# Joins between the steps of the first stage, products ahead in the opening of the product-key stage, and the states of the first batch kept on chip

## The chip, the cores and the metric

The kernel runs on one core of one Trainium2 chip. The metric is the device time of one execution in microseconds (us); the time of a kernel is the median over its runs. TensorE multiplies matrices, VectorE and ScalarE do elementwise work and reductions, GpSimd does elementwise work and issues transfers whose rows are chosen by data, SyncE (SP) issues most other transfers, and ScalarE issues some of them. All values are float32; in the profile each matrix product of the program stands as two TensorE instructions, and "products" below counts those.

## The reference

Two layers follow each other, each of the form `x = x + ffn(cond(x))`, on x of 16 batches, 256 tokens and 256 features (N = 4096 tokens). Cut to what matters here:

```python
# layer 0, cond: a shared gated net and two of eight experts for each token
shared = silu(xf @ w1) * (xf @ w3) @ w2
s = sigmoid(concat([xf, t_emb]) @ router_W)          # the two largest of s + router_bias are chosen
y0 = (shared + sum_of_two(gate * (gelu(xf @ W1e[e]) @ W2e[e]))) / 3
# layer 0, ffn: product keys, 8 heads, 8 of 64 x 64 pairs of keys for each head
xn = (y0 - mean) * rsqrt(var + eps) * gamma + beta    # mean and var over ALL tokens
sim = einsum(xn @ w_q.T, keys)                        # 2 x 8 heads x 64 scores
idx, scores = top 8 of the 64 sums of the top 8 of either half
o = gelu(y0 . key_in[idx]) * softmax(scores);  x1 = x + o @ key_out[idx]
# layer 1, cond: a recurrent net over the 256 tokens of each batch (gates i, f, o, g) -> z
# layer 1, ffn: attention on z, then two of eight experts for each token; x1 + result
```

The mean and the variance over all tokens stand between the first stage and the product keys: no choice of keys can begin before the last token of y0 is there.

## The kernel before, in words

**Order.** The Python functions are generators that emit instructions; `steps(gen, n)` lets one emit up to its n-th next `yield`. When the program is built, a scheduler fixes the order on each engine: among the instructions whose inputs and buffers it expects to be ready, it takes the one that stands earliest in the emitted text. So an instruction can run well ahead of its place in the text (the load of `gam`, line 558, left at 0.7 us), and one that stands late is put off while earlier ones keep its engine busy. On the chip each engine runs its fixed order and waits where an input is late.

**First stage (to 474.7 us).** y0 is held transposed in `y` (also called `sh`), in 8 blocks of 512 tokens. `route(c)` (line 325 on) handles 1024 tokens: the logits `lg` (335), Sigmoid (342), the choice of two experts, and 16 scattered transfers of rows to `axd` (`send`, line 323), through two buffers `row`. `shared(blk)` (416 on) computes the shared net of a block in four steps: h1 = w1 x (423), h3 = w3 x (426), Tanh (428), two VectorE instructions to `gt` (429, 431), and at once the products of `gt` with w2 into `acc` (433). Line 436 writes the result into `sh`. Routing chunk c runs beside block 2c. After the four chunks stand, in the text, the loads of gamma, beta, `kin` and `kout` (the product-key tables, 4 MB each, in four pieces each, 558 to 564, from ScalarE's queue), then `listing`, `shared(1)` and the 71 expert tiles of `routed`. Those tiles (192 to 372 us) scatter their results into `ayd`.

**Joins (371.9 to 474.7 us).** `join(blk)` (217 on) goes through the four groups of 128 tokens of a block: it loads the two expert results of each token from `ayd` (222, SP, three buffers `r`), sums them on GpSimd (224), transposes the sum (227) and adds it to `sh` (229). Then it stores the block to `yd` (232, ScalarE's queue), takes the statistics (234) and copies the first 16 tokens of each batch to `y0` (235). In the text: `shared(3)` with steps of `fold` (which prepares the keys `wk`, 584 to 590), joins 0, 1, 2, `shared(5)` with `fold`, joins 3, 4, 5, `shared(7)`, joins 6, 7.

**Product-key stage (to 2401 us).** 32 chunks of 128 tokens (8 tokens of each of 16 batches). For chunk u, `select_experts(u)` makes scores `sp` (715), the top 8 (725, 726), the pairs (738, 739), and turns the result to `chosen` (773, 777), in eight steps; `weights_of` builds the dense weights `w` of the chunk in eight steps (VectorE 793, 794, 796; TensorE 801 into the single buffer `wp`; ScalarE 805); `experts(u, w, xt)` has eight steps of 16 products `po` with `kin` (820), Gelu to `ge` (825), the multiplication with `w` (826) and 16 products `acc` with `kout` (829). `recur(v)` is the recurrent net over the eight tokens of the chunk before (897 to 916), which writes the states `zt`. `wts` has two buffers, and so have `po` and `ge`.

The opening does all of `select_experts(0)`, `weights_of` of chunk 0 and `select_experts(1)`. The loop over u then takes, eight times, one step each of `experts(u)`, `weights_of` for u + 1, `select_experts(u + 2)` and `recur(u - 1)`. Each second chunk the states go to memory, `zd` (999).

**Attention and second experts (2401 us on).** For each batch b, `front(b)` reads its states z from `zd` (1029, four buffers); `ends(b)` is the last to use them (1273, 1279).

Of the kernel before, what the change touches and what calls it, by code (L numbers as in the profile page):

```python
# [8 lines left out]
F32 = mybir.dt.float32  # L9
# [152 lines left out]
def adaln_ffn_kernel(ctx: ExitStack, tc: tile.TileContext, i: dict, out: bass.AP):  # L162
# [54 lines left out]
    def join(blk):  # L217

        for u in range(blk * TBLK // P, (blk + 1) * TBLK // P):
# [9 lines left out]
            nc.vector.tensor_tensor(sh[:, :, cols], sh[:, :, cols], pj, ALU.add)  # L229
        nb = TBLK // T  # L230
# [6 lines left out]
    with (  # L237
# [76 lines left out]
        now = {"count": count}  # L314

# [12 lines left out]
        def route(c):  # L328
# [13 lines left out]
            nc.scalar.activation(s, s, AF.Sigmoid)  # L342
# [73 lines left out]
        def shared(blk, xb=None):  # L416

            xb = xb or load_x(blk)
            acc = [pacc.tile([P, TBLK], F32, name=f"acc{d}", tag=f"acc{d}") for d in range(KC)]
            for c in range(HS // P):  # L420
                h1 = pmm.tile([P, TBLK], F32, name="h1", tag="mm")
                for k in range(KC):
                    nc.tensor.matmul(h1, w1[:, k, c * P : (c + 1) * P], xb[:, k, :], start=(k == 0), stop=(k == KC - 1))
                h3 = pmm.tile([P, TBLK], F32, name="h3", tag="mm")
# [7 lines left out]
                for d in range(KC):  # L432
                    nc.tensor.matmul(acc[d], w2[:, c, d * P : (d + 1) * P], gt, start=(c == 0), stop=(c == HS // P - 1))
                yield
            for d in range(KC):
                nc.scalar.mul(sh[:, d, blk * TBLK : (blk + 1) * TBLK], acc[d], 1.0 / 3.0)
# [121 lines left out]
        nc.scalar.dma_start(out=gam, in_=i["gamma"])  # L558
        nc.scalar.dma_start(out=bet, in_=i["beta"])
        for q in range(4):  # L560
            w = NE // 4
            nc.scalar.dma_start(out=kin[:, :, q * w : (q + 1) * w], in_=i["kinT"][:, :, q * w : (q + 1) * w])
            w = NC // 4
            nc.scalar.dma_start(out=kout[:, q * w : (q + 1) * w], in_=i["kout"][:, q * w : (q + 1) * w])
# [28 lines left out]
        with tc.tile_pool(name="cf", bufs=2) as cf:  # L593
            fd = fold(cf, ptr)
            for n, blk in enumerate((3, 5, 7)):
                sh_ = shared(blk)
                for _ in range(HS // P):
                    steps(sh_, 1)
                    steps(fd, 1 if n < 2 else 0)
                steps(sh_)  # L600
                if n == 0:
                    for b_ in (0, 1, 2):
                        join(b_)
                elif n == 1:
                    for b_ in (3, 4, 5):
                        join(b_)
            steps(fd)
            for b_ in (6, 7):
                join(b_)
# [13 lines left out]
    with tc.tile_pool(name="cw", bufs=1) as cw:  # L623
# [32 lines left out]
        lnw = fw.tile([P, 4, KC], F32, name="w_ln")  # L656
        wqk = fw.tile([P, 2, KC, D], F32, name="wqk")
        with (
# [153 lines left out]
            def experts(u, w, xt):  # L812

                acc = [pacc.tile([P, P], F32, name=f"acc{d}") for d in range(KC)]
                yu = of_tile(yt[u // XT], u % XT)
                for c in range(0, NC, CQ):
                    po = pmm.tile([P, CQ, P], F32, name="po", tag="mm")
                    for h in range(CQ):
                        for k in range(KC):
                            nc.tensor.matmul(  # L820
                                po[:, h, :].rearrange("p (b t) -> p b t", t=SPC), kin[:, k, (c + h) * P : (c + h + 1) * P], yu[:, k],
                                start=(k == 0), stop=(k == KC - 1),
                            )
                    ge = ct.tile([P, CQ, P], F32, name="ge")
                    nc.scalar.activation(ge, po, AF.Gelu)  # L825
                    nc.vector.tensor_tensor(ge, ge, w[:, c : c + CQ, :], ALU.mult)  # L826
# [93 lines left out]
            def new_w(u):  # L920
# [704 lines left out]
```

## Time and profile before

| | us |
|---|---|
| median of 3 runs | 3642.41 |
| lowest, highest | 3628.58, 3655.81 |
| profiled execution | 3655.55 |
| its span in the profile | 3653.4 |
| mean granted TensorE clock | 0.953 |

| stretch | from | to |
|---|---|---|
| routing, shared blocks 0, 2, 4, 6, 1 | 0 | 192 |
| 71 expert tiles | 192 | 371.9 |
| shared blocks 3, 5, 7, joins, keys | 371.9 | 474.7 |
| opening of the product-key stage, and chunk 0 | 474.7 | 588 |
| chunks 1 to 31 | 588 | 2355 |
| recurrent net of the last chunk, alone | 2355 | 2401 |
| attention and second experts | 2401 | 3653.4 |

How to read it: the profile is of one execution. An engine's busy share is an average over stages with different limits, so each stage is read from the wait that ends last in it. In a line of the time line stand start, length, engine, line of the kernel, operation, output<-inputs, count, and in brackets the idle time before it and what ended it. PE is TensorE, PEld its loading of weights, DVE is VectorE, ACT is ScalarE, POOL is GpSimd. A `q` behind an engine's name is its issuing of transfers. Buffer numbers are left out of names.

### The profile page before, as it was taken

To read this page: it belongs to the slowest core of one execution; us is meant where nothing else is said; L and a number is where in the kernel's file an instruction comes from. 1 tells how busy PE (TensorE), PEld (TensorE's weight loads), DVE (VectorE), ACT (ScalarE), POOL (GpSimd) and SP (SyncE) were. 2 spreads that over 40 slices of the span, in tenths; PEclk is the share of its full clock that TensorE was granted. 3 is DMA by queue.
4 is the path that set the end of the run, shared out by engine and by line. 5 is a ranking of instruction groups with operands and counts; after the bars stand their busy time and mean duration, and the time that the engine had idled before them with its cause. 6 is when DMAs were issued, how large, how long until landed. Compare 5 with 4: busy or idle time off the path is not lost.

```text
span 3653.4 us, 72829 instructions
## 1 busy us (share of the span) xinstructions
PE 3407.6 (93%) x26776; PEld 2584.4 (71%) x26776; DVE 2282.4 (62%) x7358; ACT 1492.2 (41%) x3700; POOL 669.4 (18%) x1148
## 2 busy tenths in 40 slices
PE   7899869999999999999999999869999999999896
PEld 4467447777777777777777777635577777777796
DVE  3433378888787887878888787335555646455323
ACT  1133125455454544545455454333343444443221
POOL 3545220000000000000000000101222222222221
PEclk9999969999999999999999999967799999999997
DMA  6233430111101111011111101130133333232666
GB/s 232 95 106 107 146 72 13 33 27 30 36 16 36 22 36 33 19 36 22 36 23 29 36 19 30 33 116 24 52 102 115 103 117 103 99 102 97 199 218 219
DMA packets 423359, 273.05 MB, mean 75 GB/s; under 512 B 304800, under 2 KB 381472, under 8 KB 412384
## 3 DMA queue, kind: packets, MB, share of 16 engines
q1 hardware_dynamic: 397776, 208.21, 21.1%
q0 software_dynamic: 13344, 36.60, 2.7%
q10 hardware_dynamic: 11888, 23.60, 1.9%
q8 instruction: 216, 3.54, 0.4%
q14 instruction: 135, 1.11, 0.1%
HBM read 191.88 MB, written 76.44 MB: 73 GB/s over the span
## 4 chain that ended last, share of the span: by engine, by line
PE 73%; DVE 9%; DMA 6%; issue 5%; ACT 4%; POOL 2%; SPq 0%; ACTq 0%; DVEq 0%; POOLq 0%
PE acc L829 13%; PE po L820 9%; PE gp L897 7%; PE wp L801 7%; PE g L1458 6%; PE g L1445 5%; PE sp L715 3%; PE bp L853 3%; PE sc L1209 3%; PE ph L517 2%; PE mm L1237 2%; PE py L531 2%; DVE i L726 1%; DVE s L725 1%; DMA axd<-row,slot 1%
## 5 line engine op out<-in xcount | busy, mean ns | idle before, releaser
L829 PEld LDWEIGHTS acc<-ge,kout 128*128 128x128 f32 x4096 | 485.3, 193 | 93.9 <-DVE ge L826 47.5
L820 PEld LDWEIGHTS po<-yt,kin 128*128 128x128 f32 x3840 | 458.9, 191 | 105.8 <-issue 105.0
L829 PE MATMUL acc<-ge,kout 128*128 128x128 f32 x4096 | 525.5, 281 | 6.4 <-DVE ge L826 4.9
L820 PE MATMUL po<-yt,kin 128*128 128x128 f32 x3840 | 508.0, 281 | 0.0
L805 ACT COPY wts<-wp 64x256 f32<-64x256 f32 x1024 | 375.2, 366 | 187.5 <-PE wp L801 174.9
L916 POOL TENSOR_SCALAR zt<-hT 128x32 f32<-128x32 f32 x256 | 118.9, 465 | 1530.7 <-DVE hT L915 1403.3
L897 PE MATMUL gp<-wh,hT 128*32 128x256 f32 x4096 | 318.9, 393 | 30.6 <-DVE hT L915 22.1
L796 DVE TENSOR_TENSOR oh<-chosen,parted 128x1024 f32<-128x1024 f32 x256 | 311.8, 1218 | 0.0
L801 PE MATMUL wp<-oh,ol 128*64 128x128 f32 x4096 | 300.3, 284 | 9.7 <-ACT wts L805 9.6
L1449 ACT ACTIVATE hT<-g,b 128x128 f32<-128x128 f32 x284 | 104.7, 369 | 431.4 <-DVE hT L1451 367.4
L1458 PE MATMUL g<-mw,hT 128*128 x1136 | 272.9, 395 | 6.8 <-ACT xT L1435 3.5
L1445 PE MATMUL g<-xT,w 128*128 128x128 f32 x2272 | 274.7, 276 | 1.2 <-DVE ys L1463 1.2
L1445 PEld LDWEIGHTS g<-xT,w 128*128 128x128 f32 x2272 | 269.1, 192 | 6.0 <-DVE ys L1463 1.6
L801 PEld LDWEIGHTS wp<-oh,ol 128*64 128x64 f32 x4096 | 229.6, 139 | 59.7 <-issue 15.7
L1458 PEld LDWEIGHTS g<-mw,hT 128*128 128x128 f32 x1136 | 220.9, 200 | 43.6 <-ACT xT L1435 8.5
L825 ACT ACTIVATE ge<-po 128x512 f32<-128x512 f32 x256 | 151.8, 593 | 216.2 <-PE po L820 210.6
L897 PEld LDWEIGHTS gp<-wh,hT 128*32 128x32 f32 x4096 | 119.0, 110 | 155.2 <-issue 52.4
L793 DVE TENSOR_TENSOR ol<-chosen,iota 128x512 f32<-128x512 f32 x256 | 175.2, 684 | 67.5 <-ACT chosen L777 46.6
L1209 PE MATMUL sc<-qk 32*128 32x256 f32 x2048 | 197.5, 420 | 7.3 <-DVE npads L1216 5.9
L903 ACT ACTIVATE g<-gp 128x192 f32<-128x192 f32 x256 | 84.8, 331 | 288.9 <-PE gp L897 287.5
L826 DVE TENSOR_TENSOR ge<-ge,wts 128x512 f32<-128x512 f32 x256 | 175.3, 685 | 33.0 <-ACT ge L825 29.8
L1451 DVE TENSOR_SCALAR hT<-g,b 128x128 f32<-128x128 f32 x284 | 97.0, 341 | 130.0 <-PE g L1445 76.5
(349 smaller groups left out, 5391.1 us busy)
## 6 DMA issues: line engine op xcount, KB each, us to landing
w<-in_mw SPq DMA_DIRECT2D x71, 1024.0 KB, 5.2
xwd<-xw SPq DMA_DIRECT2D x64, 256.0 KB, 4.3
xr<-xwd SPq DMA_DIRECT2D x256, 64.0 KB, 2.5
xs<-axd SPq DMA_DIRECT2D x71, 129.0 KB, 2.2
xs<-xsd SPq DMA_DIRECT2D x71, 129.0 KB, 2.1
b<-in_b SPq DMA_DIRECT2D x71, 128.0 KB, 4.3
r<-ayd SPq DMA_DIRECT2D x64, 128.0 KB, 2.7
mw<-in_mw SPq DMA_DIRECT2D x8, 1024.0 KB, 13.3
```

Of the source, the lines that this page charges most:

```text
L793: nc.vector.tensor_tensor(ol, bc(c[:, 0, g : g + GT], 2, NK), bc(iota[:, 0:NK], 1, GT), ALU.is_equal)
L796: nc.vector.tensor_tensor(oh, bc(c[:, 1, g : g + GT], 2, P), bc(parted, 1, GT), ALU.is_equal)
L801: nc.tensor.matmul(wp[half[s], t], ol[:, at, :], oh[:, at, :], start=True, stop=True)
L805: nc.scalar.copy(wr[half[h], :, :, at : at + GH], wp[half[s], :, :, h * NHI : (h + 1) * NHI].rearrange("p t r c -> p c r t"))
L820: nc.tensor.matmul(po[:, h, :].rearrange("p (b t) -> p b t", t=SPC), kin[:, k, (c + h) * P : (c + h + 1) * P], yu[:, k], start=(k == 0), s ...
L825: nc.scalar.activation(ge, po, AF.Gelu)
L826: nc.vector.tensor_tensor(ge, ge, w[:, c : c + CQ, :], ALU.mult)
L829: nc.tensor.matmul(acc[d], kout[:, c + h, d * P : (d + 1) * P], ge[:, h, :], start=(c + h == 0), stop=(c + h == NC - 1))
L897: nc.tensor.matmul(gp[j * CW : (j + 1) * CW], state["hT"][:, k, :], group(wh, k, j), start=False, stop=(k == KC - 1), skip_group_check=True,)
L1209: nc.tensor.matmul(s[j][:, t], qk[rows(j), w, c, t * P : (t + 1) * P], qk[rows(j), 1 - w, c, :], start=True, stop=True)
L1445: nc.tensor.matmul(ph[:, f], w1[n][:, k, at * P : (at + 1) * P], xT[n][:, k], start=(k == 0), stop=(k == KC - 1))
L1458: m = nc.tensor.matmul(acc, hT[n][:, f], mw2[:, bass.ds(e, 1), f].rearrange("p o d -> p (o d)"), start=(f == 0), stop=(f == NF - 1))
```

## The change

- Loads: `gam`, `bet` and `kin` are issued on ScalarE's queue only behind the Sigmoid of the second routing chunk, `kout` behind that of the third (`issue_after`); two pieces of 2 MB each instead of four of 1 MB.
- `shared`: the w2 products of a step are emitted one step later, behind the next step's h1 products; a fifth step holds the last of them.
- Joins: `join` yields after each group of 128 tokens. 26 of the 32 groups are spread over the fifteen steps of `shared(3)`, `shared(5)` and `shared(7)`, in the block order 0, 1, 2, 4, 6, 3, 5, 7; six groups follow.
- Opening: `select_experts(1)` is taken out of it. Instead all eight groups of products `po` and Gelus of chunk 0 are emitted between the weight steps of chunk 0, into a second `wts` buffer. In chunk 0, `experts` multiplies these eight pieces into `w` at once, in place, and has only the `kout` products left.
- Pace: in chunk u, what is missing of the choice for u + 1 comes first, two steps at a time (four places of eight in chunks 0 and 1, three in 2, two in 3, one in 4); the eight weight steps follow in the places that are left. Chunks 1 to 4 hold ten choice steps each, chunk 0 and those from 5 on eight. From chunk 5 on the loop emits what it did before.
- States: `z0` holds z of batch 0 on chip; GpSimd copies it from `zt` each second chunk. Its load from `zd` goes, and the other batches have three buffers instead of four.

```diff
@@ join
             nc.vector.tensor_tensor(sh[:, :, cols], sh[:, :, cols], pj, ALU.add)
+            yield
@@ shared
             for c in range(HS // P):
                 h1 = ...
+                if c:
+                    down(c - 1)
                 h3 = ...
...
-                for d in range(KC):
-                    nc.tensor.matmul(acc[d], w2[:, c, d * P : (d + 1) * P], gt, start=(c == 0), stop=(c == HS // P - 1))
+                gts[c] = gt
                 yield
+            down(last)
+            yield
@@ after the routing chunks
-        for q in range(4):
-            w = NE // 4
-            nc.scalar.dma_start(out=kin[:, :, q * w : (q + 1) * w], in_=i["kinT"][:, :, q * w : (q + 1) * w])
...
+        with tc.issue_after(marks[1]):
...
+            for q in range(2):
+                w = NE // 2
+                nc.scalar.dma_start(out=kin[:, :, q * w : (q + 1) * w], in_=i["kinT"][:, :, q * w : (q + 1) * w])
+        with tc.issue_after(marks[2]):
...
@@ joins
+            ready = joins((0, 1, 2, 4, 6, 3, 5, 7))
+            JN = 8 * TBLK // P
+            count = 0
             for n, blk in enumerate((3, 5, 7)):
                 sh_ = shared(blk)
-                for _ in range(HS // P):
+                for c in range(HS // P + 1):
                     steps(sh_, 1)
                     steps(fd, 1 if n < 2 else 0)
+                    upto = (n * (HS // P + 1) + c + 1) * (JN - 6) // 15
+                    upto = min(upto, (5 + n) * TBLK // P)
+                    steps(ready, upto - count)
+                    count = max(count, upto)
...
+            steps(ready)
@@ experts
+                if ready is not None:
+                    for c in range(0, NC, CQ):
+                        nc.vector.tensor_tensor(w[:, c : c + CQ, :], ready[:, c : c + CQ, :], w[:, c : c + CQ, :], ALU.mult)
@@ opening
             steps(select_experts(0, done))
-            w, gw = new_w(0)
-            steps(gw)
-            steps(select_experts(1, done))
+            early = new_w()
+            w = new_w()
+            gw, pre = weights_of(done[0], w), ahead(0, early)
+            for _ in range(P // 2 // GT):
+                steps(gw, 1)
+                steps(pre, 1)
@@ the loop over chunks
+                at, must, to = chosen_by(u - 1), NS * (u + 1), chosen_by(u)
+                lead = -(-max(0, must - at) // 2)
...
+                        if q < lead:
+                            steps(choices, min(2, must - at))
+                            at += min(2, must - at)
+                        else:
+                            if q == lead:
+                                gw = weights_of(done[u + 1], w)
+                            n, of = q - lead, NQ - lead
+                            steps(gw, (n + 1) * NQ // of - n * NQ // of)
+                            more = (to - at) * (n + 1) // of - (to - at) * n // of
+                            steps(choices, more)
...
                 if u > 0 and v % XT == XT - 1:
+                    nc.gpsimd.tensor_copy(z0[:, :, tiles_of(v // XT)], zt[v // XT][:, :, 0])
@@ attention
-        zs = {}
+        zs = {0: z0}
-            zs[b] = fx.tile([P, KC, T], F32, name="z", bufs=4)
+            zs[b] = fx.tile([P, KC, T], F32, name="z", bufs=3)
-        load_z(0)
         load_z(1)
```

## The prediction

> **What bounds the kernel now.** I read the page's totals and slices first.
>
> ```profile
> span 3653.4 us, 72829 instructions
> PE 3407.6 (93%) x26776; PEld 2584.4 (71%) x26776; DVE 2282.4 (62%) x7358; ACT 1492.2 (41%) x3700; POOL 669.4 (18%) x1148
> ...
> PE   7899869999999999999999999869999999999896
> ...
> PEclk9999969999999999999999999967799999999997
> ```
>
> A slice is 91 us. TensorE fills all but the first two, the fifth and sixth (365 to 548), the two from 2283 and two near the end. The change works in the first three of these places. Next, the busy time of the engines in stretches (stretch, length, then busy us of PE, PEld, DVE, ACT, POOL, the granted clock, the DMA share, GB/s).
>
> ```profile
> 465.70:474.70 9.00, 3.15 (x11) 1.40 (x11) 3.29 (x8) 0.00 (x0) 7.56 (x12) 0.60 0.95 304
> 474.70:498.90 24.20, 14.42 (x80) 11.39 (x79) 19.05 (x109) 7.27 (x11) 10.56 (x13) 0.78 0.82 107
> 498.90:533.20 34.30, 19.78 (x136) 13.19 (x136) 28.86 (x103) 13.18 (x36) 0.00 (x0) 0.60 0.16 16
> 707.20:765.00 57.80, 57.01 (x532) 43.63 (x531) 46.37 (x161) 29.14 (x79) 4.78 (x9) 1.00 0.20 33
> 2355.00:2402.00 47.00, 20.12 (x144) 6.86 (x142) 13.64 (x60) 10.53 (x36) 6.22 (x15) 0.61 0.20 40
> ```
>
> The fourth line is one chunk of the steady product-key stage: TensorE 57.0 of 57.8 us, VectorE 46.4. The opening (474.7 to 533.2) has TensorE busy for 34 of 58 us, and at a low clock. Then the chain that ended last (start, us, what).
>
> ```profile
> 31.00 7.31 DMA axd<-row,slot
> ...
> 113.00 2.83 DMA axd<-row,slot
> ...
> 681.45 2.65 PE po L820 x22
> 739.23 2.65 PE po L820 x22
> ...
> 2401.16 5.25 DMA zd<-zt
> 2406.47 2.99 DMA z<-zd
> ```
>
> A scattered row took 7.31 us while the large loads ran and 2.83 later; a chunk's period is 57.78; two transfers follow each other before attention starts. Last, TensorE's time line in the opening, and its waits from 365 to 480.
>
> ```profile
> 509.39 1.09 PE L801 MATMUL wp<-oh,ol 128*64 128x128 f32 x16 [1.60 <-ACT wts L805]
> 512.08 1.98 PE L801 MATMUL wp<-oh,ol 128*64 128x128 f32 x16 [1.60 <-ACT wts L805]
> ```
>
> ```profile
> PE pj L227 <- POOL r L224: 13.7, 9, 4.2
> ```
>
> The profiled execution took 3655.55 us for its span of 3653.4; the median of the runs is 3642.41 (3628.58 to 3655.81), 0.4% lower. I take the sum off the profiled time, and the same microseconds off the median.
>
> **Part 1, loads of kin and kout later.** Eight loads (8 MB) leave the first 50 us; four of 2 MB come behind the second and third Sigmoid. At the start, the second xb took 10.11 us to land against a median of 6.1: 4.0 at most, and I take 3, since 16 lg products of 3.55 us lie between. The sends of the first routing chunk run from 29.53 to 63.51 (34.0 us), those of the others 26.1, 24.7 and 25.4: 8.6 us. The moved loads must be paid somewhere. 50 us moved 316 GB/s, so 4 MB is an estimated 13.3 us; from Sigmoid to the first send pass 11.1 us (61.87 to 72.99) in which no row of that chunk is sent. About 2 us meet the sends, and four contended sends took 9.8 us (39.90 to 49.71) against 5.7 (114.85 to 120.51): I take half the difference, +2, in each of two chunks. Sum -7. Bounds: -12 if all is covered, +6 if both chunks become like the first (2 x 8.6). ScalarE's queue issues 4 transfers instead of 8, at 0.3 to 0.6 us each; nothing waits there. TensorE's products of `shared` lie beside this chain.
>
> [...]
>
> **Part 2, joins between the steps, `down` one step later.** No work is added: 64 row loads on SP, 32 sums on GpSimd, 64 transposes, 8 stores on ScalarE's queue move forward. Between 371.9 and 465 TensorE stood 7.2 us for joined rows (the 13.7 less 6.5 behind 465.7) and ran six products after the wait at 453 in 4.8 instead of 3.1 us: 9.0 in all. With a join about every 3.5 us and three buffers, each filled in 3.8 to 5.2 us, rows should be there: I take -8. The end stays: six joins are left behind the last products as five were, with loads of 4.4 us; block 7 needs its `shared` result anyway. Bounds: -12 (3 us of the end go too), +3 (the first joins stand before the rows of the last scatter, the first of which was summed at 381.70). `down` later removes waits on gt (3.8 at 49.57, 4.49 at 161.41) that lie beside the sends: 0; without that cover up to 8 us more.
>
> **Part 3, opening.** Before: chosen(0) at 498.9, eight weight steps to 529.9, chosen(1) at 538.97, eight more steps to 585.4, and chunk 1's first kout products at 587.97. The second choice leaves the opening; the other half of chunk 0's 128 kin products and its eight Gelus (0.60) move ahead, where TensorE has 44 of 117 us free (its 117.1 us from 474.7 to 591.8 hold 77 us of work at the mean busy times of the chunk from 765.0 to 822.7, whose 60.5 us of busy time overlap into 57.7: so about 73). Before the change, 64 of them already ran there, from 474.66 to 488.6. Now chosen(1) comes behind eight multiplications instead of one: +7 x 0.60 = 4.2, at 543. Choice 2 (14.2 us of VectorE, as choice 1: 523.60 to 537.77, less a multiplication, with xn) no longer lies between the steps of weights(1): 8 x 2.7 = 21.6, the period at 507.83 to 510.53. So 543.2 + 21.6 + 1.5 + 2.6 = 569 instead of 588: -19. Bounds: -23 if the multiplications stay behind the choice; -12 if the steps run at the slow period of 3.57 (512.08 to 515.66). I take 2.7, because chunk 0's 128 kout products (14 us) stand just ahead and keep TensorE busy; at 557.12, between products, the 16 took 1.09.
>
> The eight choice steps are made up in chunks 1 to 4: TensorE 4.0 us of sp and 0.55 of tp, of which the idle opening can take some; I charge 4. VectorE goes from 46.4 to 50 us of 57.8 per chunk, beside TensorE, so 0; if the cover goes (first the choice, then weights twice as dense, in the second half of a chunk 8 x 2.6 + 3.5 + 6.5 = 31 us of VectorE, for weights, choice and the rest, against 4 x (1.9 + 1.9 + 1.05) + 8 x 1.0 = 27 of TensorE), up to 4 us in each of four chunks. Choice 2's load of yt (6.7 us) moves with it; SP is idle from 500 to 588. Sum -15, bounds -23 to +4.
>
> For the weight steps, the row is 1.98 against 1.09 us for 16 products. [...]
>
> **Part 4, z0.** The 5.25 and 2.99 us before the first attention product go; a copy on GpSimd of about 0.3 us comes in (zt's 128x32 takes 0.32), 16 in all on an engine that is 18% busy. Next late is bqk: its last load leaves SP at 2415.40, bias was formed at 2419.09 and used at 2423.06; with one load fewer that may come 2 us earlier, so qk gains less than the first product. I take -6; bounds -8 and -2. Later z loads have three buffers; the load at 2491.81 followed the release at 2483.49 and was needed at about 2605, and now follows that of 2540.75: still 55 us early, so SP holds nothing up.
>
> **Sum.** -7 - 8 - 15 - 6 = -36: 3619.5 for the profiled execution, 3606 against the median.
>
> **Rivals.**
> A, more than forecast: weights(0) at full clock (-4.4), nothing charged in chunks 1 to 4 (-4), the joins' end 3 us shorter, part 1 fully covered (-5): 3590. For it: TensorE has the room. Against: the clock row.
> B, given back: in chunks 1 to 4 the weights come late and TensorE stands 4 us in each: +16, 3622. For it: the 31 us of VectorE in half a chunk. The same size comes from part 1 at its bad bound (+13, 3619).
> C, slower: the order inside the steady chunk shifts. Steps from chunk 5 on have the same text, but the scheduler enters them in another phase, and a chunk's 57.8 us hold 16 kout products in 1.79 or 1.98 us by their neighbours. The place is the 27 chunks from 5; at 1.33 us per chunk the gain is gone, at 2.5 it is +67: 3674. Against it: the period stayed 57.78 over all the chunks before.
> D, part 4 hidden: bqk holds attention as before, +4: 3610.
>
> **How the numbers follow.** Forecast with D 0.48 (own range 3594 to 3617), A 0.20, B 0.18, C 0.14. 1% is 36.4 us, about what a measurement of this kernel tells from no change; the forecast lies on that line, 0.28 beyond and 0.20 within. Faster: 0.28 + 0.20 = 0.48. Slower: 0.11 of C. Same: 0.41. Range 3576 to 3650: the good bounds together give 3587, less 11 for the spread of the runs (27 us in all); above, it takes in B and the milder part of C.
>
> **What would show it.** Part 1: sends of the first routing chunk in 26 us, and the second and third not over 28. Part 2: under 4 us of waits of pj before the last `shared`. Part 3: 19 us less from chosen(0) to chunk 1's first kout product, and a period of 57.8 from chunk 5. Part 4: first attention product 1 us after the last state. I am wrong if the period moves, or if chunks 1 to 4 take over 60 us each.

## The result, and the profile after the change

Medians, in us:

| | before | after | ratio, 95% interval |
|---|---|---|---|
| first set, 6 executions each | 3642.36 (3628.58 to 3655.81) | 3609.72 (3605.53 to 3615.58) | 0.9919 [0.9899, 0.9939] |
| second set, 31 and 12 executions | 3642.14 (3630.82 to 3662.16) | 3624.13 (3612.28 to 3637.72) | 0.9951 [0.9931, 0.9971] |

The change makes the kernel 18 to 33 us faster. Both ratios lie within 1% of no change and both intervals exclude 1. The second set belongs to the experiments; the profile shown here is of the first. Its execution took 3609.16 us, for a span of 3607.4. The profiled execution of before (3655.55 us) is none of its six and lies at their upper end, so that the two spans differ by 46.0 us: more than the medians do, in either set. Where these 46 us lie is the first question.

The totals of the page after the change, to be laid beside those before:

```profile
span 3607.4 us, 72831 instructions
...
PE 3373.3 (94%) x26776; PEld 2564.6 (71%) x26776; DVE 2277.7 (63%) x7358; ACT 1492.2 (41%) x3701; POOL 686.0 (19%) x1164
...
PEclk9999989999999999999999999968999999999997
```

The same 26776 products keep TensorE busy 34 us less, at a mean granted clock of 0.962 instead of 0.953. Busy time times clock is nearly the same (3373.3 x 0.962 is 3245, 3407.6 x 0.953 is 3247), so that nearly all of the 34 us is, by this estimate, time in which products ran at a lower clock. The sixth digit of the clock (the opening, 451 to 541) went from 6 to 8, which the change can have done. The 28th and 29th (2435 to 2616) went from 7 and 7 to 8 and 9, in attention, of which the change touches only the entry and the number of buffers for z.

Busy time in stretches (stretch, length, then PE, PEld, DVE, ACT, POOL, clock, DMA share, GB/s), the first from the last product of `shared` to the last joined row, the second to the first choice, the third the weights of chunk 0, the fourth chunk 5:

```profile
449.40:464.90 15.50, 6.41 (x24) 4.18 (x25) 4.96 (x12) 0.60 (x1) 12.83 (x18) 0.61 0.87 273
465.00:490.60 25.60, 9.20 (x39) 5.72 (x37) 18.76 (x109) 4.88 (x8) 7.59 (x9) 0.77 0.89 103
490.60:521.60 31.00, 29.77 (x235) 21.41 (x236) 23.05 (x50) 19.46 (x45) 0.95 (x1) 0.84 0.04 4
790.69:851.68 60.99, 60.44 (x575) 45.40 (x573) 47.74 (x163) 32.48 (x89) 5.07 (x10) 1.00 0.14 27
```

The first is the surprise: this end of the joins took 9.7 us before. In the third, TensorE is busy 29.8 of 31.0 us instead of 19.8 of 34.3. The fourth is one long chunk (57.78 before); from chunk 6 on the period is 57.7 again.

The waits of TensorE for joined rows, from 356 to 470 (us in all, times, longest):

```profile
PE pj L227 <- POOL r L224: 10.2, 6, 4.1
```

13.7 us became 10.2, and of these all but 2.3 lie behind the last product of `shared`. The chain of work that ended last, at the entry of attention:

```profile
2383.39 0.32 POOL zt L952
...
2383.76 0.22 POOL z L1067
...
2384.03 2.09 PE mm L1207 x4
```

Last state, copy to z0, first product of attention: the two transfers of before (5.25 and 2.99 us) are gone.

How far the profiled execution after is ahead of the one before, at marks that both have (x+z is the sum with which GpSimd closes a batch of attention):

| mark | before | after | ahead |
|---|---|---|---|
| first product of the routed tiles | 195.82 | 186.98 | 8.8 |
| last product of `shared` ends | 465.06 | 449.39 | 15.7 |
| last transpose of a joined row ends | 474.74 | 464.85 | 9.9 |
| x of chunk 4 is added (VectorE) | 812.70 | 790.69 | 22.0 |
| x of chunk 5 is added | 870.48 | 851.68 | 18.8 |
| last gate product ends | 2397.85 | 2381.29 | 16.6 |
| first qk product | 2419.27 | 2393.80 | 25.5 |
| first x+z of attention (GpSimd) | 2483.49 | 2457.71 | 25.8 |
| fourth x+z | 2651.12 | 2608.10 | 43.0 |
| last x+z | 3398.27 | 3352.35 | 45.9 |

17.2 us are gained between the first and the fourth batch of attention, where the change does nothing. By these marks the first and the fourth part gave more than forecast; the second gave 6.9 us and lost 5.8 of them at once.

### The profile page after: what moved, and what is told of

The parts are those of the page before. It is cut to its first block, busy times and chain, and to the rows that moved or that the text cites. A ratio compares the mean times of both kernels' runs of the same rounds, so it can differ in the third digit from the quotient of the medians.

```text
span 3607.4 us, 72831 instructions
## 1 busy us (share of the span) xinstructions
PE 3373.3 (94%) x26776; PEld 2564.6 (71%) x26776; DVE 2277.7 (63%) x7358; ACT 1492.2 (41%) x3701; POOL 686.0 (19%) x1164
## 4 chain that ended last, share of the span: by engine, by line
PE 73%; DVE 10%; issue 5%; DMA 4%; ACT 4%; POOL 2%; SPq 1%; ACTq 0%; DVEq 0%; POOLq 0%
PE acc L865 13%; PE po L839 9%; PE gp L933 7%; PE wp L822 7%; PE g L1526 6%; PE g L1513 5%; PE sc L1277 3%; PE bp L889 3%; PE sp L736 3%; PE ph L529 2%; PE mm L1305 2%; PE py L543 2%; DVE i L747 2%; DVE s L746 1%; PE mm L1241 1%
## 5 line engine op out<-in xcount | busy, mean ns | idle before, releaser
L865 PEld LDWEIGHTS acc<-ge,kout 128*128 128x128 f32 x3968 | 467.0, 192 | 86.1 <-issue 42.4
L865 PE MATMUL acc<-ge,kout 128*128 128x128 f32 x3968 | 505.5, 280 | 3.2 <-DVE ge L862 1.7
L933 PE MATMUL gp<-wh,hT 128*32 128x256 f32 x4096 | 318.3, 393 | 30.5 <-DVE hT L951 21.4
L822 PEld LDWEIGHTS wp<-oh,ol 128*64 128x64 f32 x4096 | 226.5, 137 | 57.6 <-issue 12.8
```

The lines of the kernel that those rows point to most:

```text
L822: nc.tensor.matmul(wp[half[s], t], ol[:, at, :], oh[:, at, :], start=True, stop=True)
L865: nc.tensor.matmul(acc[d], kout[:, c + h, d * P : (d + 1) * P], ge[:, h, :], start=(c + h == 0), stop=(c + h == NC - 1))
L933: nc.tensor.matmul(gp[j * CW : (j + 1) * CW], state["hT"][:, k, :], group(wh, k, j), start=False, stop=(k == KC - 1), skip_group_check=True,)
```

## The experiments

Two theories were to be told apart. *Stages*: each part acts in its own stage, by what the marks show. *Chance*: part of the marks (attention, perhaps routing) differs from one execution to the next in one and the same kernel, and belongs to no part. Each kernel was timed against the kernel before in the same set. "Later `down`" is the part of the change that emits the w2 products one step later. The table gives the marks of all profiled executions (us: first routed product; start of `shared(3)`, called the fourth shared block, to last joined row, and of it the end behind the last shared product; from there to the end of chunk 5; from there to the last gate product; from there to the first qk product; first to fourth x+z of attention).

| kernel | routed | joins | end | to chunk 5 | to last gate | to qk | four batches |
|---|---|---|---|---|---|---|---|
| before | 195.8 | 102.6 | 9.7 | 396.7 | 1526.4 | 21.4 | 167.6 |
| before, again | 196.9 | 105.5 | 9.6 | 390.4 | 1526.3 | 21.6 | 154.5 |
| part 1 alone | 201.1 | 99.1 | 10.0 | 396.6 | 1526.7 | 21.4 | 153.5 |
| part 2 alone | 197.2 | 102.1 | 15.7 | 389.9 | 1526.6 | 21.7 | 150.8 |
| part 3 alone | 201.4 | 99.6 | 10.1 | 385.0 | 1526.7 | 22.1 | 153.4 |
| part 4 alone | 196.1 | 102.4 | 9.8 | 395.1 | 1528.1 | 12.8 | 150.6 |
| after | 187.0 | 102.1 | 15.5 | 387.8 | 1528.6 | 12.5 | 150.4 |
| after, again | 195.6 | 101.7 | 15.6 | 386.9 | 1528.9 | 12.5 | 150.9 |
| after without part 1 | 200.6 | 99.7 | 15.9 | 386.4 | 1528.9 | 12.5 | 150.9 |
| after without later `down` | 199.9 | 97.6 | 15.5 | 387.5 | 1528.7 | 12.5 | 168.3 |
| after without part 2 | 200.1 | 103.1 | 9.9 | 385.6 | 1528.1 | 12.5 | 164.6 |
| first hold | 196.1 | 97.0 | 13.3 | 387.2 | 1528.6 | 12.5 | 168.3 |
| second hold | 191.7 | 98.0 | 15.5 | 384.5 | 1529.3 | 12.6 | 150.9 |
| third hold | 196.8 | 95.4 | 13.4 | 386.2 | 1528.0 | 12.5 | 151.7 |

**Part 1 alone.**

```diff
+            marks.append(nc.scalar.activation(s, s, AF.Sigmoid).ins)
...
+        with tc.issue_after(marks[1]):
...
+                nc.scalar.dma_start(out=kin[:, :, q * w : (q + 1) * w], in_=i["kinT"][:, :, q * w : (q + 1) * w])
```

> The kernel before with the later loads of kin and kout alone. Theory of stages (each part acts in its own stage, and the stages add): the first product of the routed tiles comes at 187 instead of 195.8 us, everything behind it is moved by these 9 us, and the kernel takes 9 us less. Rival, contention moved: the third routing chunk, where kout now lands, grows from 32 to 36 us or more, and no more than 5 us are left. Rival, chance of the clock: the first four attention batches (first to fourth x+z on GpSimd: 167.6 us before, 150.4 in the changed kernel, same products) take another time here too, although nothing near them is changed.

Ratio 0.9974 [0.9955, 0.9993], that is 7 us off 3645.95. The first routed product came at 201.1, later than in the kernel before, so the theory of stages fails here: the sends of the first routing chunk took 24.2 us (34.0 before), those of the next two 28.2 and 30.3 (26.1 and 24.7 before), so that 7.7 of the 9.8 us come back there. So the 7 us off the whole time are not seen in routing, nor behind it: against before again it is 495.6 to 495.9 us from the fourth shared block to the end of chunk 5, and 1548.1 to 1547.8 from there to the first qk product. Where they lie stays open. The four batches took 153.5 us though nothing near them was touched.

**Part 2 alone.**

```diff
+                if c:
+                    down(c - 1)
...
+                    steps(ready, upto - count)
```

> The kernel before with the joins between the steps and the later down products alone. Theory of stages: from the start of the fourth shared block to its last product 86.6 instead of 92.9 us, but from there to the last transpose of a joined row 15.5 instead of 9.7, so less than 1 us net, and the same time as before. Rival: the long end belongs to the new opening (wx and wh loads and their scaling placed among the last joins), so that without it the end stays at 9.7 and the kernel takes 6 to 8 us less. Rival, chance of the clock: the first four attention batches take another time than 167.6 us.

Ratio 0.9988 [0.9967, 1.0009]. The end of the joins took 15.7 us with the old opening too, so the rival is out. The stretch from the last joined row to the end of chunk 5 was 389.9, just under the 390.4 to 396.7 of the four kernels without parts 2 and 3. From the fourth shared block to the end of chunk 5 it took 491.9 us, where those four have 495.6 to 499.4. Whether the opening's work that was moved into the end pays there was not tried.

**Part 3 alone.**

```diff
-            steps(select_experts(1, done))
...
+                steps(gw, 1)
+                steps(pre, 1)
```

> The kernel before with the new opening and the pacing of the choices alone. Theory of stages: at the end of chunk 4 it is 12 us ahead and at the end of chunk 5 9 us, as in the changed kernel, and it takes 9 us less. Prediction on record: 15 us less, 19 at chunk 1's first kout product. Rival: with the joins of the kernel before, wx and wh lie elsewhere and nothing is paid in the joins' end, so 15 us are seen. Rival, chance of the clock: the first four attention batches take another time than 167.6 us.

Ratio 0.9985 [0.9966, 1.0003]. The stretch from the last joined row to the end of chunk 5 took 385.0; in the four kernels without parts 2 and 3 it is 390.4 to 396.7, with a mean of 394.7: 9.7 us less. Stages, not the 15 on record.

**Part 4 alone.**

```diff
+                    nc.gpsimd.tensor_copy(z0[:, :, tiles_of(v // XT)], zt[v // XT][:, :, 0])
...
+        zs = {0: z0}
```

> The kernel before with the states of batch 0 kept on chip alone (and three buffers for z). Theory of stages: the first attention product follows the last state 9 us earlier (2.8 instead of 11.7 us behind the last gate product), the first four attention batches stay near 167.6 us, and the kernel takes 9 us less. Rival: the shorter attention batches of the changed kernel (150.4 us) come from this part, by the way in which attention is entered; then the kernel takes 25 us less. Rival, chance of the clock: those batches take a time between without relation to this part, and differ as much in the kernels with part 1, 2 or 3 alone.

Ratio 0.9996 [0.9973, 1.0019]: the whole time does not resolve this part. Its stage does: from the last gate product to the first qk product 12.8 us instead of 21.4 to 22.1 in the five kernels without it, and some 2 us are paid ahead of it (1528.0 to 1529.3 from chunk 5 to the last gate product in the nine kernels with part 4, 1526.3 to 1526.7 in the five without). The four batches took 150.6, with part 2 or 3 alone 150.8 and 153.4: the shorter batches are not this part's. Most of the 2 us lie in the recurrent net of the last chunk. There VectorE's constants for attention come earlier, in before and in the changed kernel:

```profile
2398.05 0.97 DVE L1054 TENSOR_SCALAR below<-iota,pid 128x128 f32<-128x128 f32 x1
```

```profile
2338.68 0.90 DVE L1122 TENSOR_SCALAR below<-iota,pid 128x128 f32<-128x128 f32 x1
```

Before, they stood behind the last gate product, and the last state came 3.3 us after it (2.4 in the changed kernel). With this part they stand behind the x of chunk 31, among the first steps of the net, and from that x to the last gate product it takes 43.9 to 44.7 us instead of 42.4 to 42.6. The traces show the place; no run held the constants back.

**The changed kernel again** (no edit).

> The changed kernel once more. Theory, chance of the clock in attention and a real gain in routing: the first four attention batches take 148 to 156 us as in five of the six kernels so far, the first product of the routed tiles comes at 187, within 3 us, and the kernel takes 0.9 to 1.0% less than before. Rival, routing by chance too: that product comes anywhere between 187 and 201 us (187.0 in the changed kernel, 201.1 with part 1 alone), and the gain is smaller by as much.

Ratio 0.9951 [0.9931, 0.9971]. First routed product at 195.6, not 187.0: of the 8.8 us in the first table most can be chance, and the rival holds. The four batches took 150.9.

**Without the later down products**, joins as changed.

```diff
-                if c:
-                    down(c - 1)
+                for d in range(KC):
+                    nc.tensor.matmul(acc[d], w2[:, c, d * P : (d + 1) * P], gt, start=(c == 0), stop=(c == HS // P - 1))
```

> The changed kernel with the down products put back behind their own gt, the joins as changed. Theory: the later loads pay only together with the later down products, because otherwise TensorE stands on gt ahead of the router's products (second Sigmoid at 53.9 instead of 50.0, third chunk of sends 10 us after the second); then the first routed product comes at 198 to 202 instead of 187, and 12 us of the gain are lost. Prediction on record: the later down products are worth 0, with up to 8 us if their cover goes. Rival, chance: the product comes at 187, within 4 us, and the time is that of the changed kernel.

Ratio 0.9960 [0.9942, 0.9978]. First routed product at 199.9. With later loads and without later `down`, all three kernels have it at 199.9 to 201.1; with both, all five at 187.0 to 196.8. The time line of TensorE shows one way in which they are tied, first of part 1 alone, then of the changed kernel:

```profile
46.60 3.78 PE L434 MATMUL acc<-gt,w_w 128*128 128x512 f32 x4 [3.44 <-DVE gt L432]
50.17 3.42 PE L336 MATMUL lg<-w_router_w,xb 128*128 128x8 f32 x16
```

```profile
46.07 1.98 PE L427 MATMUL acc<-gt,w_w 128*128 128x512 f32 x4
47.89 1.85 PE L337 MATMUL lg<-w_router_w,xb 128*128 128x8 f32 x16
```

In the first, the router's products for the next chunk stand in TensorE's order behind a w2 product that waits 3.44 us for gt, and then take 3.42 us. In the second they follow at once and take 1.85, at a mean clock of 1.00. But the second Sigmoid of the other kernels with both came at 51.1 to 55.1, against 53.8 to 54.0 without `down`; the two groups part only between the second and the fourth Sigmoid (71.4 to 75.1 us against 78.0 to 80.1). That the pair belongs together is shown by the marks of these eight executions; that this one wait is all of it is not, and the whole time (0.9960 beside 0.9951) does not show the 12 us that the theory had.

**Without part 2.**

```diff
-                    steps(ready, upto - count)
...
+                if n == 0:
+                    for b_ in (0, 1, 2):
+                        join(b_)
```

> The changed kernel without part 2 (no joins between the steps, no later down products). Theory of interference: with the new opening the joins between the steps are worth nothing or less, since the end behind the last shared product grows by 5.5 and the first choice comes 2.4 later; from the start of the fourth shared block to the end of chunk 5 it takes 485 to 488 us against 489.9, while the first routed product comes at about 200 for lack of the later down products: together 8 to 12 us more than the changed kernel. Prediction on record: part 2 is worth 8 us in the join stage and 0 in routing, so 498 from the fourth block to the end of chunk 5, first routed product at 187.

The later `down` is out as well. Ratio 0.9964 [0.9944, 0.9984], where the changed kernel has 0.9951 in the same set. From the fourth shared block to the end of chunk 5 it took 488.8 us, and part 3 alone 484.6; the three kernels with all of parts 2 and 3 took 489.9, 488.5 and 486.1. So next to the new opening the joins between the steps show no gain, and the 8 us on record are refuted there; with the old opening part 2 alone had 491.9 against 495.6 to 499.4.

**First hold.** wx and wh are kept behind the last joins.

```diff
+            with tc.issue_after(final["load"]):
+                for n, gate in enumerate(ORDER):
+                    nc.sync.dma_start(out=wx[:, :, n], in_=i["wx"][:, :, gate * D : (gate + 1) * D])
...
+            with tc.issue_after(final["sum"]):
+                for k in range(KC):
```

> The changed kernel with the loads of wx and wh on SyncE queued behind the last load of joined rows, and their scaling on GpSimd behind the last sum of joined rows. Theory: it is this work that lengthens the end of the joins from 9.7 to 15.5 us; held back, the end takes 9 to 11 us, and the kernel 4 to 6 us less than the changed one. Rival, store and loads: the end waits for the rows' transfers, which share the DMA engines with the store of y (1 MB) and for three buffers; then the end stays at 14 to 16. Second rival: the end is shorter, but wx, wh and what is queued behind them on SyncE (yt for chunk 2) come later and the opening gives the 5 us back.

Ratio 0.9940 [0.9917, 0.9964]. The end shrank from 15.5 to 13.3 us, less than expected, and the second rival holds in another form: the first choice product came 8.5 us behind the last joined row instead of 5.7. VectorE's time line (the lines around the first choice's shift):

```profile
471.59 0.17 DVE L698 RECIPROCAL amp<-amp 128x2 f32<-128x2 f32 x1 [0.51 <-ACT amp L697]
475.76 0.11 DVE L1004 MEMSET hT<- 128x64 f32 x1 [4.00 <-DMA yd<-y]
475.79 0.12 DVE L699 TENSOR_TENSOR amp<-amp,gam 128x2 f32<-128x2 f32 x1
```

A memset whose tile TensorE first reads at 582.62 stands 4.0 us, by the profile for the store of y, and the amplitude that the first choice needs is queued behind it. The same memset waited 1.38 us for that store in the changed kernel, and in the kernel before 2.15, by the profile for a load of the gate biases.

**Second hold.** All of the recurrence's preparation is kept back, the memsets too, and the early po products behind the last transpose of a joined row.

```diff
+            with (
+                tc.issue_after(final["load"]), tc.issue_after(final["sum"]),
+                tc.issue_after(final["pair"]), tc.issue_after(final["tp"]),
+            ):
```

> The changed kernel with all work of the recurrence's preparation held back: its loads behind the last load of joined rows, GpSimd's scaling and memsets behind the last sum, VectorE's memsets of hT and g behind the pair sums of the first choice, TensorE's first gate products behind the first choice's transposes, and the early po products behind the last transpose of a joined row. Theory: with the loads and the scaling alone held back, the end of the joins was 13.3 instead of 15.5 us, and then VectorE stood 4.0 us in the memset of hT, which waits for the store of y, ahead of the shift that the first choice needs. With that moved as well: end of the joins 9.5 to 11 us, first choice product within 4 us of it (5.7 to 8.5 so far), and from the start of the fourth shared block to the end of chunk 5 476 to 481 us, against 484.3 to 489.9; the kernel takes about 0.8% less than before. Rival: the rows' loads and the store of y (1 MB) set the end, so it stays at 13 us or more, or the late wx and wh make the solo steps of the recurrence or chunk 1 wait, and 484 is seen again.

Ratio 0.9912 [0.9893, 0.9931]. The first choice product came 5.5 us behind the last joined row, with the memset out of the way (8.5 in the first hold). But the end took 15.5 again: into the gap on SyncE the scheduler put two loads of x, which move 256 KB each in pieces of 64 bytes (8559 of the 12297 packets between 448 and 470 us have under 512 bytes; in the end of the changed kernel 319 of 3930 have). From the fourth shared block to the end of chunk 5 it took 482.5, between theory and rival.

**The kernel before again** (no edit).

> The kernel before once more. Theory, chance: the first four attention batches have two ways to go, near 151 or near 168 us, whatever the kernel (167.6, 168.3, 168.4 and 164.6 against 150.4 to 153.5 so far); a second execution of the kernel before has either, and the first routed product comes at 195 to 202. A value near 151 in this kernel would show that the 17 us belong to no part of the change; one near 168 leaves that to the kernels with all parts, which had both.

Ratio 0.9992 [0.9975, 1.0009]. The four batches took 154.5 us in the kernel before: the 17 us need no part of the change. The stretch from the second x+z to the third, in the same columns as above, in before, in before again and in the first hold:

```profile
2540.75:2598.72 57.97, 54.24 (x285) 34.14 (x284) 29.01 (x74) 20.96 (x37) 10.76 (x18) 0.74 0.14 46
```

```profile
2530.91:2581.38 50.47, 45.21 (x283) 29.16 (x283) 28.89 (x74) 21.13 (x38) 10.78 (x18) 0.88 0.16 53
```

```profile
2522.34:2580.30 57.96, 54.24 (x285) 34.15 (x284) 29.09 (x74) 20.86 (x37) 10.77 (x18) 0.74 0.14 46
```

The same products (285, 283 and 285 of them are recorded) keep TensorE busy 54.2 or 45.2 us, at a mean clock of 0.74 or 0.88; the busy times of VectorE, ScalarE and GpSimd agree to 0.3 us. Four of the fourteen profiled executions have four batches of 164.6 to 168.3 us, ten of 150.4 to 154.5, and the kernel before has both kinds. The changed kernel had the short one twice, three of its variants the long one.

**The change without part 1.**

```diff
-        with tc.issue_after(marks[1]):
...
+        for q in range(4):
+            w = NE // 4
+            nc.scalar.dma_start(out=kin[:, :, q * w : (q + 1) * w], in_=i["kinT"][:, :, q * w : (q + 1) * w])
```

> The changed kernel with kin and kout loaded at the start again. Theory: the later loads and the later down products pay together, 5 us in routing: first routed product at 196 to 201 here against 187.0, 195.6 and 196.1 with both; the kernel takes 0.4% less than before. Rival: the down products alone bring it, and the first routed product comes at 193 or sooner. Prediction on record: 7 us later than the changed kernel, which by the mean of its three profiles, 192.9, is 199.9.

Ratio 0.9949 [0.9932, 0.9966], first routed product at 200.6: as the theory had it in the mark. The whole time is no worse than that of the changed kernel in the second set (0.9951), so that the 4 to 5 us of routing are not confirmed by it.

**Third hold.** The loads of x are held back too.

```diff
+                        with tc.issue_after(final["load"]):
+                            nc.sync.dma_start(out=xt[u // XT], in_=i["xT"].rearrange("p k (b t) -> p k b t", t=T)[:, :, :, tiles_of(u // XT)])
```

> The kernel of the last hold with the loads of x for the product-key stage held behind the last load of joined rows too. In that kernel two of these loads (256 KB each, in 64-byte pieces) stood among the last loads of joined rows on SyncE, and the last seven sums each waited 0.3 to 2.1 us for their rows. Theory: without them the end of the joins is 9.5 to 12 us instead of 15.5, from the start of the fourth shared block to the end of chunk 5 it takes 477 to 480 us instead of 482.5, and the kernel takes 0.9 to 1.1% less than before. Rival: the rows of the last joins and the stores of y (512 KB each) fill the DMA engines by themselves; then the end stays at 14 us or more, as in every kernel with joins between the steps, and nothing is gained on the last hold.

Ratio 0.9905 [0.9878, 0.9932], 3615.33 against 3651.05. The end took 13.4 us: 2.1 less than in the changed kernel, as in the first hold, and not the 9.5 to 12 expected. GpSimd's wait for rows in the end of this kernel (us, times, longest), and its group of wx scalings in the end of the changed kernel:

```profile
POOL r L226 <- DMA r<-ayd: 6.5, 5, 1.8
```

```profile
L995 POOL TENSOR_SCALAR wx<-wx 128x256 f32<-128x256 f32 x4 | 3.4, 849 | 0.0
```

With the scalings gone (3.4 us for wx, 3.3 for wh) the sums wait 6.5 us for their rows, with the DMA engines busy 86% of the time at 259 GB/s. So about 2 us of the longer end are the opening's work on GpSimd. The rest goes with a count. GpSimd's sums of joined rows in the end, in before (465.06 to 474.74) and in the changed kernel (449.4 to 464.9):

```profile
L224 POOL TENSOR_TENSOR r<-r 128x256 f32<-128x256 f32 x5 | 3.5, 722 | 0.3 <-DMA r<-ayd 0.2
```

```profile
L224 POOL TENSOR_TENSOR r<-r 128x256 f32<-128x256 f32 x7 | 5.0, 720 | 1.7 <-DMA r<-ayd 1.7
```

Seven groups are left behind the last product of `shared` in all eight kernels with joins between the steps, held or not, and five in the six others. Five in 9.7 us and seven in 13.4 are both 1.9 us for a group, so that two groups more are an estimated 3.8 of the 5.8 us. What sets the time of a group differs: the sums of before hardly wait for rows, those of the third hold do, by these waits for the transfers of the last rows beside the stores of y. No run left five groups or took those stores away, so that this is argued and not shown. The stretch to the end of chunk 5 took 481.6 us against 486.1 to 489.9 in the changed kernels. This version is the best of the study in the ratio, but its interval overlaps both of the changed kernel's: the 6.6 us are seen in the stage and not proved in the time.

## Why the prediction was right, and where it was not

The time on record (3606) is 4 us from the first median and 18 from the second; the range holds both. The sum behind it (-36) was too large. By the means of the table, the parts have in their stages:

- Part 1 with the later `down`: first routed product at 197.6 on the mean of four kernels without either, 193.4 on the mean of five with both: -4.1, forecast -7.
- Parts 2 and 3, from the fourth shared block to the end of chunk 5: 497.1 on the mean of the four kernels without them, 488.2 on the mean of the three with all of both: -8.9, forecast -8 and -15.
- Part 4, from the end of chunk 5 to the first qk product: 1548.2 on the mean of the five kernels without it, 1541.1 on the mean of the nine with it: -7.1, forecast -6.

Together -20.1, where the two measurements have -32.6 and -18.0. The two first traces differ by more, 46.0 us, and much of that lies where the executions of one kernel differ too: 17 us in attention, up to 9 in routing. Why all six executions of that set lie near or below the fastest of the second set (3605.5 to 3615.6 against 3612.3 to 3637.7) stays open; their mean granted clock was 0.961 against 0.959, which by the 3.0 us for 0.001 in the last section is an estimated 7 of the 14 us between the medians.

**Part 1.** The stated sign held in the first trace: the first routing chunk sends for 25.6 us, the second for 27.5, the third for 27.6. In the changed kernel again and the three holds the third took 28.8 to 30.7, over the 28 that were named. The sign was also too narrow; between the chunks, and with `down` in its old place, the gain is lost. The step that failed is "from Sigmoid to the first send pass 11.1 us (61.87 to 72.99) in which no row of that chunk is sent", from which +2 per chunk followed. From the second Sigmoid to the fourth it takes 67.9 to 69.0 us in the four kernels without either edit, 71.4 to 75.1 with both and 78.0 to 80.1 with the loads alone: 2 to 12 us given back, where the forecast had 4. Of the 7 us forecast 4.1 remain, though the means are of marks that scatter by 5 to 10 us. The 3 us of the start are there in every trace: the first Sigmoid comes at 13.7 to 14.0 us in the eight kernels with later loads and at 16.4 to 17.1 in the six without. Costing `down` at 0 was wrong as well: its waits do not lie beside the sends once the loads are late.

**Part 2.** The term was right where it was worked out, and the step beside it failed. The joins' waits ahead of the last product of `shared` went, and the block of products took 86.6 us instead of 92.9: 6.3 of the 8 forecast, and 2.3 us of waits were left ("under 4"). "The end stays: six joins are left behind the last products as five were" was wrong. It takes 9.6 to 10.1 us in the six kernels without joins between the steps and 15.5 to 15.9 in all five with them and no hold. The prediction gave a sixth group no time, and the traces have seven against five. Nor did it ask what else would run there: in the first two traces eight of the opening's scalings stand among the sums instead of five, with its loads and first products. That work held back was worth 2.1 us; the two groups are the larger share by the estimate above.

**Part 3.** From chosen(0) to chunk 1's first kout product it takes 77.6 us (490.64 to 568.27) instead of 89.1: -11.4, forecast -19. Even this flatters the part, for the 89.1 from which the prediction set out is the long one of two courses. The five kernels with the old opening take 89.1, 88.9 and 87.7 us, where the clock stands at one half until 549 to 554 us (511.8 to 552.8 in before), and 81.8 and 80.2, where it is back at 542.2 and 538.4; the nine with the new opening take 75.7 to 78.9. By the means, 85.5 and 76.9, that is -8.6. Two terms of the prediction were too small. The first is chosen(1), forecast 4.2 us later for seven more multiplications; from chosen(0) to chosen(1) it went from 40.1 to 48.4, +8.3. VectorE's time line, before and after:

```profile
523.60 0.35 DVE L725 MAX8 s<-sim 128x8 f32<-128x64 f32 x2
...
537.41 0.36 DVE L770 TENSOR_TENSOR tr<-pe,ps 128x64 f32<-128x64 f32 x2
```

```profile
515.26 0.34 DVE L746 MAX8 s<-sim 128x8 f32<-128x64 f32 x2
...
520.46 4.90 DVE L854 TENSOR_TENSOR wts<-wts 128x512 f32<-128x512 f32 x8 [3.15 <-ACT wts L826]
526.19 0.60 DVE L728 TENSOR_SCALAR xn<-yt,amp,shift 128x128 f32<-128x128 f32 x2 [0.83 <-PE sp L736]
...
537.61 0.35 DVE L791 TENSOR_TENSOR tr<-pe,ps 128x64 f32<-128x64 f32 x2
```

Before, VectorE made choice 1 in one run of 14.2 us, beside the last weight steps of TensorE and ScalarE (to 529.9). Now it breaks off after a few of its steps, waits 3.15 us for ScalarE's last copy of weights(0), multiplies for 4.90, waits 0.83 for products that TensorE made late, and goes on: 22.7 us. The prediction counted the multiplications and not that they wait for the end of the weights, which the choice had not. The second is weights(1): from chosen(1) to the end of the last copy 27.3 us (539.02 to 566.31), forecast 23.1. The first copy came 4.6 us behind the choice, and of the seven periods after it two were slow ones, 3.58 and 3.57, and one took 3.31. The clock in weights(0) was better than forecast:

```profile
500.91 1.09 PE L822 MATMUL wp<-oh,ol 128*64 128x128 f32 x16
501.94 1.38 PE L839 MATMUL po<-y,kin 128*128 128x128 f32 x10
503.61 1.09 PE L822 MATMUL wp<-oh,ol 128*64 128x128 f32 x16 [0.29 <-ACT wts L826]
```

The po products were placed between the weight steps, and seven of eight steps took 1.09 us, where five of these had taken 1.98. In all nine kernels with the new opening the last five steps took 1.09 or 1.10, in the five with the old one the last four 1.97 or 1.98. Before, the clock fell to one half at 511.8 us, where the gaps between the steps were 1.60 us. No run varied these gaps alone, so what brings the clock down or back there was not shown. The full clock gained little, for the first two steps came 5.5 us apart and the whole went from 31.0 to 29.8 us. Of the charge for chunks 1 to 4 (+4), 3.2 us are paid, all in chunk 5 (60.99 us).

**Part 4.** The mechanism was right. The first product comes 2.7 us behind the last gate product (11.7 before) and 0.3 behind the last state; forecast was 1. The doubt about bqk was not borne out: the first qk product gains 8.9 as the first product does, and rival D is out. Not foreseen are the 2 us that the kernels with this part lose ahead of it, most of them in the recurrent net of the last chunk.

**Rivals.** A: the clock in weights(0) came as it said. Its 4.4 us, an estimate of five steps at 1.09 instead of 1.98 us, are shown by no run; weights(0) became 1.2 us shorter, by the two traces. Chunk 5 paid 3.2 us where it had nothing; the joins and routing did not come as it said. B: chunks 2 to 4 have the old period (57.4 to 57.8), and what is given back is 3.2 us in chunk 5. C is refuted: from the end of chunk 5 to the last gate product all fourteen kernels took 1526.3 to 1529.3 us.

## What to carry to other kernels

When a wait is taken away, ask what the scheduler will put in its place: more of the next stage's preparation stood among the last joins, two more joins were left behind the last product, and most of the wait came back there under another name. When work is moved ahead, ask not only how long it is but what it waits for; eight multiplications of 4.9 us came with a choice 8.3 us later, because part of a choice that had run beside the last weights now stands behind them. And judge a part by marks that enclose its own stage, in several executions, before its gain is read off two traces: 17 of the 46 us between these two lay in a stage that the change had left as it was, at a mean clock of 0.77 before and 0.88 after.

## What the runs showed of the hardware

The clock in attention took two courses in the fourteen profiled executions. In windows of 3.41 us at the end of the second batch of the first hold (the clock is the last number but two):

```profile
2508.69:2512.10 3.41, 2.77 (x22) 2.04 (x24) 3.41 (x5) 0.00 (x0) 0.00 (x0) 1.00 0.00 0
2512.10:2515.51 3.41, 2.36 (x15) 1.20 (x12) 3.41 (x5) 0.00 (x0) 1.44 (x2) 1.00 0.00 0
2515.51:2518.92 3.41, 3.41 (x17) 1.95 (x17) 1.98 (x4) 1.76 (x4) 1.04 (x1) 0.80 0.00 0
2518.92:2522.33 3.41, 3.41 (x9) 2.70 (x8) 0.88 (x2) 1.70 (x2) 0.00 (x0) 0.50 0.00 0
```

TensorE idles 0.64 and 1.05 us of two windows, in gaps of at most 0.64, and the clock then falls to one half. (16 router products took 3.58 us at 87.65 in the kernel before, at a clock of 0.50, and the 16 shown above 1.85 in the changed kernel, at 1.00.) In this course the stretch from the second x+z to the third takes 57.9 to 58.0 us, in four executions; in the other ten it takes 50.4 to 51.8. No gap of TensorE in this batch is longer than 0.66 us. The kernel before had both courses, with four batches of 167.6 us and of 154.5. What decides the course was not shown, and it was not controlled in any run.

The granted clock also orders the executions of one kernel. In one set the kernel before ran 35 times, in 3629.8 to 3664.0 us at mean clocks of 0.961 to 0.951; a straight line through them falls by 3.0 us for each 0.001 of clock.
